# Moving the fourth attention element, the turned attention and two groups of transfers earlier or later in a hand-ordered graph network kernel

## The chip, the core and the metric

The kernel runs on one core of a Trainium2 chip. The core has a matrix engine (TensorE; PE in the profile, with its weight loads as PEld), three engines for elementwise work (VectorE or DVE, ScalarE or ACT, GpSimd or POOL) and SyncE (SP), whose queue issues every transfer of this kernel to 16 DMA engines. The engines run side by side and wait for one another through semaphores. Each queue takes its instructions strictly in program order, so an instruction that waits holds up everything behind it on that queue.

The metric is the device time of one execution in microseconds. The kernel before took 2347.32 us (median of 3 runs, 2341.13 to 2347.89).

## The reference: what is computed

The input x is 128 elements of 128 nodes with 512 features, and adj is one 128x128 matrix for all of them. Two layers are applied, both float32:

```python
# layer 0: normalise, graph convolution, residual
h = max(layernorm(x), 0)
x = x + norm_adj @ (h @ W0) + b0          # norm_adj: adj scaled by rsqrt of its row sums, both sides
# layer 1: normalise, attention with 8 heads of 64, residual
h = max(layernorm(x), 0)
q, k, v = h @ Wq + bq, h @ Wk + bk, h @ Wv + bv
scores = q @ k.T / 8 + (1 - adj) * -1e9
x = x + softmax(scores) @ v @ Wo + bo
```

## The kernel before, in words

**Groups and stages.** The 128 elements are cut into 32 groups of four (`GB`, `NG`). The kernel is a software pipeline over stages t. A stage has five blocks of TensorE work in this order: W (layer 0's weight product of group t+1), Q, K and V (the three projections of group t), and Y (the output projection of group t-1). Each block is a 512x512x512 product made by Strassen's scheme as seven smaller products, some of them split by a second Strassen level (`Projection.step`, L553). The seven give the places of a block their names: `Q0` to `Q6`. Between the seventh product of K and the first of V, at place `V0`, stand the attention products of group t-1 (`attend`, L929, elements in the order 2, 3, 0, 1) and the scores of group t (`scores`, L855, order 0, 1, 3, 2).

**The plan.** `at(stage, place, f, ...)` puts a step on a list, and `block` (L1146) runs the lists: steps of place `Q0` come ahead of that product, `Q0b` after the product and the reads that belong to its `step`, `Q0c` after the rest of its reads. The program order so made is the order on every queue. A place says nothing of time by itself: a step that is issued by SP or ACT runs when its queue reaches it and its semaphores are there.

**Operands of a product.** Strassen needs sums of blocks. `output_operands` (of the attention's output, tile `op_o`), `attention_operands` (of the second layer's h, `op_h`) and `gcn_operands` (of layer 0's, `op_a`) make them on POOL: four operations of 128x512 (L411 to L414) and nine of 128x256 (L94), some 11.7 us together. TensorE cannot go on to the second product of a block before the first of the small ones are done.

**Attention.** Element b of a group goes through these steps: scores with the mask added by DVE (element 3 instead is copied by ACT, L869, and masked by POOL, `add_mask`, L880); `row_max` (DVE, L884, 1.2 us); `exponentials` (ACT, L896, eight heads in two halves); `softmax_end` (a reciprocal on DVE, L901, and a multiplication on POOL, L907, 1.9 us). The weights are then transposed in two steps. `flip_att` (L909) transposes 32x32 squares on DVE (1.25 us) and writes 512 KB to DRAM in one transfer (`turned<-att`, L915). `turn_att` (L917) reads them back in four transfers of 128 KB in rows of 128 bytes (`att<-turned`, L786), which puts the squares in their places. SP may not issue these four before the write has landed. Five buffers hold all this: element b's weights go to the buffer of scores b-1, and its turned form to that of b-2, so element 0's turned form takes the buffer of element 3's scores and its flip waits for element 3's exponentials.

**The second layer's h** goes the same way: `flip_h` (L767) for elements 0 and 1 and for 2 and 3, one write each (`turned_h<-att`, `turned_h<-op_o`), and `turn_h` (L777). The second write leaves from slots 28 to 35 of tile `op_o`, which `output_operands` overwrites with its small operations.

**Weights** do not all fit: the four prepared weights (q, k, v, o) lie in DRAM and are loaded again in each stage into two buffers, five transfers of 512 KB each (`reload_w`, L1115, with places from `reloads_of`, L1128). In the block named by the key, the weights for the block after the next one are loaded.

**The last and first stages** have columns of their own in the list of steps (L975): `first` for t = 1, `final` for t = 31, `place` for t = 2 to 30. In stage 31 there is no W block on TensorE, so its places all come directly after Y.

Of the kernel before, what the change touches and what calls it, by code (L numbers as in the profile page):

```python
# [97 lines left out]
def kernel(  # L98
# [19 lines left out]
    H = 8  # L118
# [47 lines left out]
    def source(g, half):  # L166
        return staged.get((g, half)) if (g, half) in staged else xts[g, half]
# [507 lines left out]
    def ln1(g, half, js=(0, 1), ready=None):  # L675

        if (g, half) not in scale1:
            scale1[g, half] = Norm(source(g, half), f"1_{g}_{half}", g > 2)
        for j in js:
            scale1[g, half].statistics(j)  # L680
        if ready is None or ready:
            scale1[g, half].scale(ready or js)
# [282 lines left out]
    def at(slot, place, f, *args):  # L965
        plan.setdefault((slot, place), []).append((f, *args))

    for t in range(-1, NG + 1):
# [3 lines left out]
        if 0 <= t - 1 < NG - 1:  # L972
            g = t - 1

            for first, final, place, f, *args in (  # L975
                ("W4", "Q0b", "Q0b", flip_att, 0),
                ("W6", "Q2b", "Q3", turn_att, 0),
                ("Q3", "Q2", "Q2c", flip_att, 1),
                ("Q5", "Q4", "Q5", turn_att, 1),
                ("W6", "-Y3", "W2", exponentials, 2, 0, H // 2),  # L980
                ("Q1c", "-Y4", "W3", exponentials, 2, H // 2, H),
                ("Q4c", "-Y5b", "W4b", softmax_end, 2),
                ("Q6c", "-Y5", "W5", exponentials, 3, 0, H // 2),
                ("K0c", "-Y6", "W6", exponentials, 3, H // 2, H),
                ("K2c", "Q0b", "Q1c" if t == 2 else "Q0b", softmax_end, 3),
                ("K1", "Q3", "Q4b", flip_att, 2),
                ("K3", "Q4b", "Q5", flip_att, 3),
                ("K3", "Q5", "K0", turn_att, 2),
                ("K5", "Q6", "K1", turn_att, 3),
            ):  # L990
                place = first if t == 1 else final if last else place
                if f in (flip_att, turn_att) and turned_in_place(g, args[0]):
                    continue
                at(t - place.startswith("-"), place.strip("-"), f, g, *args)
            if t == 1:
                at(1, "K4", transpose_att, g, 2)
                at(1, "K5", transpose_att, g, 3)
            for b in (2, 3, 0, 1):
                at(t, "V0", attend, g, b)
        if t == 0:  # L1000

            at(0, "Q0b", ln2, 1, 0)
            at(0, "Q1b", ln2, 1, 1)
            at(0, "K6", norm_h, 1, 0)
            at(0, "K6", norm_h, 1, 1)
            at(0, "V4", transpose_h, 1, 0)
            at(0, "V4", norm_h, 1, 2)
            at(0, "V5", transpose_h, 1, 1)
            at(0, "V5", norm_h, 1, 3)
            at(1, "W0", transpose_h, 1, 2)  # L1010
            at(1, "W1", transpose_h, 1, 3)
            at(1, "W1b", attention_operands, 1)
            at(2, "Q5", attention_residual, 1, 0)
            at(2, "K1", attention_residual, 1, 1)
        elif 1 <= t + 1 < NG and t >= 0:
            g = t + 1
            at(t, "Q3b" if g < NG - 1 else "Q0b", ln2, g, 0)
            at(t, "K0b" if g < NG - 1 else "Q3b", ln2, g, 1)
            if g == NG - 1:

                places = ("Q3", "Q4", "Q5", "Q5", "Q6", "Q6", "K1", "K2", "K2")
                steps = ((norm_h, 0), (norm_h, 1), (transpose_h, 0), (norm_h, 2), (transpose_h, 1), (norm_h, 3))
                steps += ((transpose_h, 2), (transpose_h, 3))
            else:
                places = ("K1c", "K2c", "K4c", "K5b", "K3", "K4b", "K6b", "V0b", "Y5")
                if t == 1:
                    places = ("K2c", "K3c", "K6", "K6b", "K4b", "K5b", "V0b", "V0b", "Y5")
                steps = ((norm_h, 0), (norm_h, 1), (norm_h, 2), (norm_h, 3))
                steps += tuple((flip_h, b) for b in range(GB))
                for half in range(2):  # L1030
                    at(t, ("V3", "Y0")[half], turn_h, g, half)
            for place, (f, b) in zip(places, steps):
                at(t, place, f, g, b)
            at(t, places[8], attention_operands, g)
            at(t + 1, "Q3", attention_residual, g, 0)
            at(t + 1, "Q4", attention_residual, g, 1)
# [2 lines left out]
            at(t, "Y3" if t == NG else "Q3" if last else "W3", store_half, t - 2, 1)  # L1039
        if 3 <= t + 2 < NG:  # L1040
            at(t, "W0b" if t > 1 else "W0", load_x, t + 2, (0,), t > 1)
            at(t, "W1" if t > 1 else "W0", load_x, t + 2, (1,), t > 1)
        if 2 <= t + 2 < NG:
            g = t + 2
            if t > 0:
                at(t, "Q0b", ln1, g, 0, (0,), ())
                at(t, "Q1c", ln1, g, 0, (1,), (0, 1))
                at(t, "Q3b", ln1, g, 1)
            places = (("Q3", "Q5"), ("Q3", "Q6"), ("Q5b", "K1"), ("Q6", "K2"))
            if t == 1:  # L1050
                places = (("Q4", "K0"), ("Q4", "K1"), ("K0b", "K2"), ("K1b", "K3"))
            for b, (norm, mix) in enumerate(places):
                at(t, norm, gcn_norm, g, b)
                at(t, mix, gcn_mix, g, b)
            at(t, "K2" if t > 1 else "K4" if t > 0 else "V1b", gcn_operands, g)
            at(t, "Q6" if t > 1 else "Y1" if t > 0 else "K3", gcn_residual, g, 0)
            at(t, "K1" if t > 1 else "Y2" if t > 0 else "K3", gcn_residual, g, 1)
        if 0 <= t < NG:
            g = t
            for b in (0, 1, 3, 2):  # L1060
                at(t, "V0", scores, g, b)
            if t > 0:
                at(t, "V0c", output_operands, t - 1)
            at(t, "V1b", row_max, g, 0)
            at(t, "V3b", exponentials, g, 0, 0, H // 2)
            at(t, "V4b", exponentials, g, 0, H // 2, H)
            at(t, "V6", softmax_end, g, 0)
            if last:
                at(t, "V5b", row_max, g, 1)
                at(t, "V5b", exponentials, g, 1, 0, H // 2)  # L1070
                at(t, "V6", exponentials, g, 1, H // 2, H)
                at(t, "Y1b", softmax_end, g, 1)
                at(t, "Y2", transpose_att, g, 0)
                at(t, "Y4", transpose_att, g, 1)
            else:
                if t > 0:
                    at(t, "V3b", row_max, g, 1)
                    at(t, "Y1", exponentials, g, 1, 0, H // 2)
                    at(t, "Y2", exponentials, g, 1, H // 2, H)
                    at(t, "Y4", softmax_end, g, 1)  # L1080
                else:
                    at(t, "V4b", row_max, g, 1)
                    at(t + 1, "W2", exponentials, g, 1, 0, H // 2)
                    at(t + 1, "W3", exponentials, g, 1, H // 2, H)
                    at(t + 1, "Q1c", softmax_end, g, 1)
                at(t, "V6b", row_max, g, 2)
                at(*((t, "Y1") if t > 0 else (1, "Q3")), add_mask, g, 3)
                at(*((t, "Y3b" if g == NG - 2 else "Y6b") if t > 0 else (1, "Q5b")), row_max, g, 3)
        if last:
            g = t  # L1090
            at(t, "Y0", row_max, g, 2)
# [36 lines left out]
    def reloads_of(t):  # L1128

        when = {  # L1130
            "Q": ((t, "K2"), (t, "K2"), (t, "K2"), (t, "K2"), (t, "K3")),
            "K": ((t, "K5"), (t, "V0"), (t, "V0"), (t, "V0"), (t, "V0")),
            "V": ((t, "V3"), (t, "Y0"), (t, "Y0"), (t, "Y0"), (t, "Y3")),
            "Y": ((t, "Y4"), (t + 1, "W2"), (t + 1, "W2"), (t + 1, "W2"), (t + 1, "W3" if t + 1 < NG - 1 else "Q2c")),
        }
        if t == 1:

            when["K"] = ((1, "V0"),) * len(PARTS)
        for kind in "QKVY":
            if kind in "QKV" and t == NG:  # L1140
                continue
            reading[0] += 1
            for part, place in enumerate(when[kind]):
                at(*place, reload_w, reading[0] + 2, part)
# [10 lines left out]
    def prologue():  # L1155
# [71 lines left out]
        at(1, "Q3c", combine_w, "o", nc.gpsimd)  # L1227
        at(1, "Q5", combine_inner, "o", nc.gpsimd)
        at(1, "K3", keep_w, "o", (slice(0, 16), slice(16, SLOTS)))
        at(1, "K3", keep_w, "k")  # L1230
        at(1, "W0c", output_bias)
        at(1, "K1c", attention_residual, 0, 0)
        at(1, "K2c", attention_residual, 0, 1)

    with tc.manual_schedule(
        engines={
# [64 lines left out]
```

## Time and profile before

| quantity | value |
|---|---|
| median of 3 runs | 2347.32 us |
| the profiled execution, its own time | 2345.87 us |
| span of its profile | 2344.1 us |
| granted TensorE clock, mean | 0.993 |
| TensorE busy | 2232.0 us, 95% |
| VectorE, GpSimd, ScalarE busy | 80%, 80%, 55% |
| DMA: moved, rate | 599.23 MB, 256 GB/s |
| DMA: share of 16 engines, the kernel's own queue | 86.8% |
| median time from issue to landing: turned<-att, att<-turned, turned_h<-op_o, w<-wd_o | 4.1, 4.1, 8.9, 11.4 us |

How to read it: the span is from the first to the last instruction of the program, and the run's own time lies 1.8 us above it. A busy engine is one that executes, and an idle one is only of interest if the end waits for it. TensorE's 112 us without work are spread over 32 stages of about 71.5 us. The list of waits says who waited for whom. The timeline of SP says when transfers are issued: its rows show descriptors being made, not the data moving, and the landing comes some microseconds later. A table of stretches of the span (windows) gives the busy time of every engine and the share of the 16 DMA engines in each stretch.

### The profile page before, as it was taken

Reading aid. Unit: us, or ns where it says so; the run is one execution under the profiler, and the core shown is the slowest. Engines: PE = TensorE matmul, PEld = TensorE weight load, DVE = VectorE, ACT = ScalarE, POOL = GpSimd, SP = SyncE. Lnnn points to the kernel's source line nnn. Section 1 sums busy time; section 2 is a strip of 40 time slices with the busy share of each in tenths; the row PEclk is TensorE's granted clock in tenths of the full one; section 3 lists DMA queues with packets and bytes.
Section 4 is the critical chain, followed back from the end, with each engine's and each line's share of the span. In section 5 each row is a group of like instructions: output and inputs, shape, how many; then the busy total and the mean of one; then the engine's idle time right before and its main releaser. Section 6 shows DMA issues by size and latency. Waiting matters only on the chain.

```text
span 2344.1 us, 78627 instructions
## 1 busy us (share of the span) xinstructions
PE 2232.0 (95%) x31597; PEld 1885.5 (80%) x31597; DVE 1886.2 (80%) x4248; ACT 1290.9 (55%) x3821; POOL 1864.7 (80%) x1993
## 2 busy tenths in 40 slices
PE   9989999999999999999999999999999999999988
PEld 7778888888878888888888888888788888888777
DVE  7778887888888788888788887888788888878775
ACT  4556654665645655546656456565466564565434
POOL 7887978779878788788787787887887977877844
PEclk9999999999999999999999999999999999999999
DMA  5488899899899998899898898899999998998884
GB/s 155 142 276 257 240 284 290 249 259 263 259 284 286 241 281 239 273 289 265 251 264 252 282 286 241 276 240 275 291 255 263 261 256 280 289 251 270 225 240 146
DMA packets 908109, 599.23 MB, mean 256 GB/s; under 512 B 765665, under 2 KB 772961, under 8 KB 907105
## 3 DMA queue, kind: packets, MB, share of 16 engines
q1 hardware_dynamic: 907744, 594.20, 86.8%
q8 instruction: 250, 4.10, 0.7%
q14 instruction: 115, 0.93, 0.1%
HBM read 455.68 MB, written 138.41 MB: 253 GB/s over the span
## 4 chain that ended last, share of the span: by engine, by line
PE 53%; DMA 10%; POOL 9%; SPq 8%; DVE 8%; ACT 7%; issue 4%; POOLq 0%; DVEq 0%
PE bank_a L142 20%; PE bank_d L142 11%; SPq L786 8%; PE bank_c L142 6%; DMA turned_h<-op_o 6%; PE bank_b L142 6%; POOL op_o L94 4%; DMA att<-turned 4%; ACT q L808 3%; PE bank_d L865 3%; DVE v L478 3%; PE pa L142 2%; ACT unused L339 2%; PE po L940 2%; ACT unused L340 1%
## 5 line engine op out<-in xcount | busy, mean ns | idle before, releaser
L896 ACT ACTIVATE att<-att,nmx 128x128 f32<-128x128 f32 x1024 | 406.9, 504 | 230.5 <-DVE nmx L884 228.3
L94 POOL TENSOR_TENSOR op_o<-op_o 128x256 f32<-128x256 f32 x297 | 212.3, 739 | 211.4 <-DMA turned_h<-op_o 115.8
L142 PE MATMUL bank_a<-op_h,w 128*64 128x256 f32 x2976 | 355.1, 381 | 11.6 <-ACT q L808 11.6
L142 PEld LDWEIGHTS bank_a<-op_h,w 128*64 128x64 f32 x2976 | 206.1, 137 | 100.3 <-ACT q L808 18.6
L478 DVE TENSOR_TENSOR xt<-xt,bank_d 128x512 f32<-128x512 f32 x610 | 269.7, 467 | 11.8 <-PE bank_d L142 0.8
L907 POOL TENSOR_TENSOR att<-att,rsm 128x1024 f32<-128x1024 f32 x121 | 228.5, 1898 | 17.6 <-DVE rsm L901 14.7
L142 PE MATMUL bank_d<-op_h,w 128*64 128x128 f32 (+1 forms) x3424 | 221.7, 275 | 0.0
L94 POOL TENSOR_TENSOR op_a<-op_a 128x256 f32<-128x256 f32 x279 | 197.4, 731 | 15.1 <-ACT v L822 5.4
L808 ACT ACTIVATE q<-bank_a,bqk 128x256 f32<-128x256 f32 x192 | 79.7, 466 | 235.2 <-PE bank_a L142 235.1
L896 ACT ACTIVATION_READ_ACCUMULATOR att<-att,nmx 128x1 f32 x1024 | 208.2, 203 | 0.0
L142 PEld LDWEIGHTS bank_d<-op_h,w 128*64 128x64 f32 x3424 | 195.1, 137 | 6.7 <-issue 0.2
L94 POOL TENSOR_TENSOR op_h<-op_h 128x256 f32<-128x256 f32 x270 | 191.0, 731 | 9.4
L872 DVE SCALAR_TENSOR_TENSOR att<-bank_d,msk 128x512 f32<-128x512 f32 x128 | 82.4, 686 | 127.0 <-PE bank_d L865 127.0
L142 PE MATMUL bank_a<-w,op_o 128*64 128x256 f32 x1536 | 182.6, 380 | 0.0
L371 ACT ACTIVATE h<-xt,nb,rs 128x512 f32<-128x512 f32 x142 | 173.4, 1226 | 16.4 <-POOL nb L356 14.7
L142 PE MATMUL bank_a<-w,op_h 128*64 128x256 f32 x1488 | 178.0, 381 | 0.0
L142 PE MATMUL bank_a<-w,op_a 128*64 128x256 f32 x1488 | 176.5, 379 | 0.0
L493 DVE TENSOR_TENSOR xt<-bank_a,xt 128x512 f32<-128x512 f32 x252 | 166.5, 681 | 3.0 <-PE bank_a L142 3.0
L142 PE MATMUL bank_d<-w,op_o 128*64 128x128 f32 (+1 forms) x1768 | 127.9, 279 | 36.9 <-POOL op_o L94 36.8
L822 ACT COPY v<-bank_a 128x512 f32<-128x512 f32 x96 | 56.2, 585 | 180.0 <-PE bank_a L142 143.7
L884 DVE TENSOR_REDUCE nmx<-att 128x8 f32<-128x1024 f32 x128 | 153.9, 1203 | 0.0
L914 DVE STREAM_TRANSPOSE att<-att 128x1024 f32<-128x1024 f32 x122 | 152.5, 1250 | 1.5 <-ACT att L896 1.2
(198 smaller groups left out, 5916.5 us busy)
## 6 DMA issues: line engine op xcount, KB each, us to landing
w<-wd_v SPq DMA_DIRECT2D x155, 512.0 KB, 6.0
w<-wd_o SPq DMA_DIRECT2D x155, 512.0 KB, 11.4
w<-wd_q SPq DMA_DIRECT2D x150, 512.0 KB, 5.3
w<-wd_k SPq DMA_DIRECT2D x150, 512.0 KB, 8.6
turned<-att SPq DMA_DIRECT2D x122, 512.0 KB, 4.1
att<-turned SPq DMA_DIRECT2D x488, 128.0 KB, 4.1
out_dram<-xt SPq DMA_DIRECT2D x62, 512.0 KB, 6.0
op_h<-turned_h SPq DMA_DIRECT2D x232, 128.0 KB, 5.2
```

Of the source, the lines that this page charges most:

```text
L94: engine.tensor_tensor(twice(out), twice(x), twice(y), ALU.subtract if minus else ALU.add)
L142: nc.tensor.matmul(out[y : y + P // 2], lhsT[:, y : y + P // 2], rhs, **flags)
L371: nc.scalar.activation(dst, src, AF.Relu, bias=nb[:, j : j + 1], scale=rs[:, j : j + 1])
L478: nc.vector.tensor_tensor(dst, dst, src, f)
L493: nc.vector.tensor_tensor(t, src.rearrange("p (r f) -> p r f", r=2), t, ALU.add)
L786: nc.sync.dma_start(dst[:, :, y * 32 : (y + 1) * 32], rows[y])
L808: nc.scalar.activation(dst[:, r], src[:, r], AF.Identity, bias=bqk[:, i, oc : oc + 1], scale=1.0)
L872: nc.vector.scalar_tensor_tensor(dst, pss[p], SCALE, mask, ALU.mult, ALU.add)
L884: nc.vector.tensor_reduce(nmx, att_of(g, b), AX.X, ALU.max, negate=True)
L896: nc.scalar.activation(dst, src, AF.Exp, bias=nmx[:, h : h + 1], scale=1.0, accum_out=sm[:, h : h + 1])
L907: engine.tensor_tensor(att, att, rsm.unsqueeze(2).to_broadcast([P, H, P]), ALU.mult)
L914: nc.vector.transpose(dst, weights_of(g, b).rearrange(order, i=4))
```

## The change

For t = 2 to 30 (the column `place`) the change moves these steps; for t = 31 (the column `final`) most of them go earlier still.

- Element 3 of a group: its mask on POOL from Y1 to V4, its row maxima on DVE from Y6b (Y3b in stage 30) to Y2b, its exponentials from W5 and W6 to Y5 and Y6 of the stage before, its softmax end from Q0b to W2. Element 2's exponentials and softmax end also move from W places to Y places.
- The turned attention: flips from Q0b, Q2c, Q4b, Q5 to W0c, Q0b, Q2c, Q4b, and turns from Q3, Q5, K0, K1 to W2, Q2, Q4, Q6. On SP the order of writes (w) and turns (T) was w0 w1 T0 w2 T1 w3 T2 T3, and is now w0 T0 w1 T1 w2 T2 w3 T3, where w0 and T0 come ahead of the k weights.
- The second write of h (`flip_h` of element 3) from V0b to K6b, ahead of the scores on DVE, and on SP ahead of four of the five transfers of o's weights, which go from V0 to V0c.
- The k weights from W2 and W3 to W3 and W6, both loads of x to W0b, and `attention_operands` from Y5 to Y6b.
- In Q, one normalisation goes from Q3 to Q3b, one mix from Q5 to Q5b and one group's statistics from Q3b to Q3c.
- At the start: half 1 of group 3 takes its statistics on DVE rather than ACT, the prepared k weights are saved at Q6 rather than K3, and group 0's second residual bias is added (on DVE) at V4b and V5b rather than K1c and K2c.

```diff
-            scale1[g, half] = Norm(source(g, half), f"1_{g}_{half}", g > 2)
+            scale1[g, half] = Norm(source(g, half), f"1_{g}_{half}", g > 3 or g == 3 and half == 0)
...
             for first, final, place, f, *args in (
-                ("W4", "Q0b", "Q0b", flip_att, 0),
-                ("W6", "Q2b", "Q3", turn_att, 0),
-                ("Q3", "Q2", "Q2c", flip_att, 1),
-                ("Q5", "Q4", "Q5", turn_att, 1),
-                ("W6", "-Y3", "W2", exponentials, 2, 0, H // 2),
-                ("Q1c", "-Y4", "W3", exponentials, 2, H // 2, H),
-                ("Q4c", "-Y5b", "W4b", softmax_end, 2),
-                ("Q6c", "-Y5", "W5", exponentials, 3, 0, H // 2),
-                ("K0c", "-Y6", "W6", exponentials, 3, H // 2, H),
-                ("K2c", "Q0b", "Q1c" if t == 2 else "Q0b", softmax_end, 3),
-                ("K1", "Q3", "Q4b", flip_att, 2),
-                ("K3", "Q4b", "Q5", flip_att, 3),
-                ("K3", "Q5", "K0", turn_att, 2),
-                ("K5", "Q6", "K1", turn_att, 3),
+                ("W4", "-Y6b", "W0c", flip_att, 0),
+                ("W6", "W0", "W2", turn_att, 0),
+                ("Q3", "W0b", "Q0b", flip_att, 1),
+                ("Q5", "W4", "Q2", turn_att, 1),
+                ("W6", "-Y3", "-Y3", exponentials, 2, 0, H // 2),
+                ("Q1c", "-Y4", "-Y4", exponentials, 2, H // 2, H),
+                ("Q4c", "-Y5b", "-Y5b", softmax_end, 2),
+                ("Q6c", "-Y5", "-Y5", exponentials, 3, 0, H // 2),
+                ("K0c", "-Y6", "-Y6", exponentials, 3, H // 2, H),
+                ("K2c", "W0", "W2", softmax_end, 3),
+                ("K1", "Q0b", "Q2c", flip_att, 2),
+                ("K3", "Q1", "Q4", turn_att, 2),
+                ("K3", "Q2", "Q4b", flip_att, 3),
+                ("K5", "Q3", "Q6", turn_att, 3),
             ):
...
-                places = ("K1c", "K2c", "K4c", "K5b", "K3", "K4b", "K6b", "V0b", "Y5")
+                places = ("K1c", "K2c", "K4c", "K5b", "K3", "K4b", "K6b", "K6b", "Y6b")
...
-            at(t, "W1" if t > 1 else "W0", load_x, t + 2, (1,), t > 1)
+            at(t, "W0b" if t > 1 else "W0", load_x, t + 2, (1,), t > 1)
...
-                at(t, "Q3b", ln1, g, 1)
-            places = (("Q3", "Q5"), ("Q3", "Q6"), ("Q5b", "K1"), ("Q6", "K2"))
+                at(t, "Q3c", ln1, g, 1)
+            places = (("Q3", "Q5b"), ("Q3b", "Q6"), ("Q5b", "K1"), ("Q6", "K2"))
...
-                at(*((t, "Y1") if t > 0 else (1, "Q3")), add_mask, g, 3)
-                at(*((t, "Y3b" if g == NG - 2 else "Y6b") if t > 0 else (1, "Q5b")), row_max, g, 3)
+                at(*((t, "V4") if t > 1 else (1, "Y1") if t > 0 else (1, "Q3")), add_mask, g, 3)
+                at(*((t, "Y2b") if t > 1 else (1, "Y3b") if t > 0 else (1, "Q5b")), row_max, g, 3)
...
-            "K": ((t, "K5"), (t, "V0"), (t, "V0"), (t, "V0"), (t, "V0")),
+            "K": ((t, "K5"), (t, "V0c"), (t, "V0c"), (t, "V0c"), (t, "V0c")),
...
-            "Y": ((t, "Y4"), (t + 1, "W2"), (t + 1, "W2"), (t + 1, "W2"), (t + 1, "W3" if t + 1 < NG - 1 else "Q2c")),
+            "Y": ((t, "Y4"), (t + 1, "W3"), (t + 1, "W3"), (t + 1, "W3"), (t + 1, "W6" if t + 1 < NG - 1 else "Q2c")),
...
-        at(1, "K3", keep_w, "k")
+        at(1, "Q6", keep_w, "k")
...
-        at(1, "K1c", attention_residual, 0, 0)
-        at(1, "K2c", attention_residual, 0, 1)
+        at(1, "V4b", attention_residual, 0, 0)
+        at(1, "V5b", attention_residual, 0, 1)
```

More of the change, by code (lines that the diff above doesn't have):

```diff
@@ L1024 @@
             else:
-                places = ("K1c", "K2c", "K4c", "K5b", "K3", "K4b", "K6b", "V0b", "Y5")
+                places = ("K1c", "K2c", "K4c", "K5b", "K3", "K4b", "K6b", "K6b", "Y6b")
                 if t == 1:
-                    places = ("K2c", "K3c", "K6", "K6b", "K4b", "K5b", "V0b", "V0b", "Y5")
+                    places = ("K2c", "K3c", "K6", "K6b", "K4b", "K5b", "V0b", "V0b", "Y6b")
                 steps = ((norm_h, 0), (norm_h, 1), (norm_h, 2), (norm_h, 3))
@@ L1131, in reloads_of @@
             "Q": ((t, "K2"), (t, "K2"), (t, "K2"), (t, "K2"), (t, "K3")),
-            "K": ((t, "K5"), (t, "V0"), (t, "V0"), (t, "V0"), (t, "V0")),
+            "K": ((t, "K5"), (t, "V0c"), (t, "V0c"), (t, "V0c"), (t, "V0c")),
             "V": ((t, "V3"), (t, "Y0"), (t, "Y0"), (t, "Y0"), (t, "Y3")),
-            "Y": ((t, "Y4"), (t + 1, "W2"), (t + 1, "W2"), (t + 1, "W2"), (t + 1, "W3" if t + 1 < NG - 1 else "Q2c")),
+            "Y": ((t, "Y4"), (t + 1, "W3"), (t + 1, "W3"), (t + 1, "W3"), (t + 1, "W6" if t + 1 < NG - 1 else "Q2c")),
         }
         if t == 1:
-            when["K"] = ((1, "V0"),) * len(PARTS)
+            when["K"] = ((1, "V0c"),) * len(PARTS)
         for kind in "QKVY":
```

## The prediction, as it stood before the result was known

> **What bounds the kernel now.** I read the list of waits first, restricted to TensorE (columns: engine and tile <- who ended the wait: us in total, times, longest).
>
> ```profile
> PE po L940 <- DMA att<-turned: 40.1, 25, 5.9
> PE bank_d L142 <- POOL op_o L94: 36.8, 53, 7.5
> PE bank_a L142 <- ACT q L808: 11.6, 29, 2.4
> PE po L940 <- POOL op_a L94: 8.9, 5, 2.2
> ```
>
> The reader is to see three stalls that recur in every stage: attention waits for its turned weights (rows 1 and 4 are the same stall under two names, 49.0 us), Y1 waits for op_o (36.8), Q5 for q's read (0.33 each). A stage takes 71.5 us (28 stages, t = 3 to 30, between the landings of the last turned transfer), so TensorE alone would need some 68.5.
>
> Then the chain of waits around one stage, for what ends the first stall:
>
> ```profile
> 1073.43 3.80 DMA att<-turned
> 1077.23 0.35 issue
> 1077.58 1.09 PE po L940 x16
> ...
> 1145.16 3.32 DMA att<-turned
> ```
>
> The turned transfer lands at 1077.23, the next stage's at 1148.48, and TensorE starts at once behind it. So I look at what holds the transfers: the busy times in three stretches of this stage (last two columns: share of 16 DMA engines, GB/s).
>
> ```profile
> 1077.00:1124.00 47.00, 45.81 (x660) 39.11 (x662) 37.98 (x83) 21.30 (x84) 38.30 (x40) 1.00 0.97 322
> 1124.00:1128.00 4.00, 3.98 (x64) 3.35 (x60) 3.93 (x10) 2.59 (x6) 2.88 (x4) 1.00 0.16 63
> 1128.00:1148.00 20.00, 18.73 (x276) 15.91 (x272) 17.03 (x45) 16.41 (x32) 17.59 (x21) 1.00 0.96 178
> ```
>
> This is the main reading: the DMA engines are full for 47 us (weights, h, x, stores) and for the last 20 us (turned attention). A stage has about 4 us in which they rest, because SP stands at flips that DVE has not made yet. SP's timeline of the stage before shows the order in the last stretch (start, length of issue; x2 in the first row is the writes at 1050.10 and 1055.97):
>
> ```profile
> 1050.10 6.19 SPq L915 DMA_DIRECT2D turned<-att  x2
> 1056.39 3.14 SPq L786 DMA_DIRECT2D att<-turned  x4
> 1059.63 2.17 SPq L915 DMA_DIRECT2D turned<-att  x1
> 1061.91 3.12 SPq L786 DMA_DIRECT2D att<-turned  x4
> 1065.13 0.77 SPq L915 DMA_DIRECT2D turned<-att  x1
> 1065.99 8.19 SPq L786 DMA_DIRECT2D att<-turned  x8
> ```
>
> From the second row on a turn never stands right behind its own write; another turn lies between and covers the write's landing. The changed order does put each turn directly behind its write. The trace has that order once, in stage 1, with the DMA share of the pause in it:
>
> ```profile
> 113.51 3.05 SPq L786 DMA_DIRECT2D att<-turned  x4
> 116.66 0.67 SPq L915 DMA_DIRECT2D turned<-att  x1
> 120.33 3.33 SPq L786 DMA_DIRECT2D att<-turned  x4
> ...
> 119.50:121.50 2.00, 2.00 (x28) 1.50 (x26) 2.00 (x3) 0.00 (x0) 1.81 (x4) 1.00 0.08 27
> ```
>
> One pair takes 120.33 - 113.51 = 6.82 us, of which the DMA engines rest some 1.9 (0.08 busy in 2.0): SP can't issue the turn before the write has landed, and nothing else is in the queue.
>
> **The change part by part.**
>
> *Turned attention, one place sooner.* SP's order w0 w1 T0 w2 T1 w3 T2 T3 becomes w0 T0 w1 T1 w2 T2 w3 T3; w0 and T0 also pass a store and four k transfers. Behind a waiting turn stand on SP: behind T0 that store and the k transfers, behind T1 and T2 the next write, behind T3 v's five transfers; these land 2 to 8 us after the last turn, as before, and V's first product, at +6.7, wants the first of them, so they keep their cover. I count from the landing of the last turned transfer. From there to the landing of the last k transfer DMA work is continuous: median 46.5 us over the 28 stages (44.6 to 48.0 but for stage 30, which has no x to load). Into it goes the first pair, behind x, so it shifts the k transfers by 6.82. w1 is in the queue behind them (its flip, at Q0b, is done at about +44, the queue gets to it at +53), and three more pairs follow. Sum: 46.5 + 4 x 6.82 = 73.8 us, +2.3 on 71.5. By bounds: a pair can't be shorter than a write into an empty queue (1050.10 to its landing, 3.1) plus the issue of its turn (3.15), 6.25, which gives 71.5; at the second pair of stage 1 the last part landed 6.05 after its issue began, with 1.15 for the write 7.2, which gives 75.3. I take 6.82, the only one measured whole. Times 28: +64, ends 0 and +106.
>
> TensorE meanwhile needs 71.5 less the attention stall (1.5 a stage) less most of the next item, 69.5. So the stall that the change attacks comes back at the same instruction: attention of element 3 waits for the last turn, now 4 us a stage instead of 1.5.
>
> *h's second write ahead of o's weights.* The flip (0.70) moves on DVE ahead of the scores, where DVE idles 3.98 us (1006.37 to 1010.34). The write enters the queue after one o transfer instead of five, and lands four times 1.28 = 5 us sooner, at about +12.5. POOL is through L414 at +10.1 and needs 3.5 more for the five operations that Y1 wants at +19. POOL's wait (7.8 us in this stage) falls to 2.4, Y1's stall of 1.05 a stage is gone. o's last four transfers land 1.3 later, at +17.6, ahead of Y1. Cover: worth 1.05 x 28 = 29 if TensorE were the bound; behind a DMA bound, nothing.
>
> *Element 3's mask, maxima, exponentials.* Nothing is added. The mask (POOL, 2.38) ends at 1025.2 in the shown stage, ahead of its reader; queued behind it is element 0's softmax end, which nothing wants before W0c. The maxima (DVE, 1.21) now stand at Y2b, directly ahead of the four reads of bank d that end at 1032.16; TensorE writes bank d again from 1032.12. Late next is therefore bank d at Y4, by some 0.7 us a stage (1.21 less 0.4 to 0.6 of slack): that gives back two thirds of the 1.05. The first flip at W0c takes the place that the maxima leave at Y6b (1.25 for 1.21). ACT has 7.73 idle ahead of element 3's exponentials, so they cost nothing sooner. `attention_operands` comes behind element 2's softmax end, from 1036.58 to about 1038.9; its first five small operations end at 1047.8, and Q1 wants them at 1049; cover 1.2 us, and what it slips beyond falls on TensorE.
>
> *k transfers at W3 and W6, x at W0b.* The x loads keep their order on SP. k's last transfer lands at about +53, K0 begins at +55 and wants only the first part, which did not move: cover 2 us for K0, 4 for K1.
>
> *Q3b, Q5b, Q3c.* Element 0's mix (16 matmuls, 0.87) leaves its place ahead of Q5's product. Before, TensorE did it and then waited 0.33; now q's read is 0.8 earlier but the product waits for it in the open: 0.1 slower to 0.3 faster a stage, taken as 0.
>
> *Start.* Saving k's weights (13.5 us in the queue) moves from 137.8 to about 124, into a time when SP idles (126.3 to 135.8), so h's second write in stage 1 lands before 163.4 and Y1's 7.46 us stall there goes, with up to 3 us of half clock behind it; between -11 and 0 (if POOL's save is what SP waits for), taken as -8. Two statistics go from ACT (0.63 + 0.72 each) to DVE (0.66 + 0.18 each), two residual biases move on DVE: between -2 and +2, taken as 0.
>
> *Stage 31.* Its W places come at once after Y, so the pairs start at about 2254 and run one behind the other: w0 lands 2257, T0, w1, three k transfers (to 2268), T1, w2 lands 2273.5, T2, w3 2280.5. The last k transfer stands at Q2c behind T2 and w3 and lands at about 2282, where before it landed at 2272.3 and cost TensorE 2.5 us. So K4 waits 12 us. T3 lands at 2286.4 and is then hidden, so the 5.87 and 1.61 of attention and their slow clock go. Net: +2, between -12 (k in time) and +6.
>
> *Sum* against the profiled execution: 2345.9 + 64 - 8 + 2 = 2404; the median of the runs is 1.4 higher: 2405.
>
> **A rule against the rows.** The Trainium skill, page "Perfetto Trace Analysis", section "Identifying the Most-Contended Engine", takes the engine with the highest occupancy and for DMA the utilization of HBM. Against the page's 358 GB/s the measured 256 are 72%, under the 80% of TensorE's weight loads, so by the rule TensorE is the bound, both stalls are gain, and the sum would be some 2284 (rival 1). I go by the rows: 0.97 in 47 us.
>
> The second is the page "TensorE: Matmul & The Clock Gate": a gap beyond about 3.4 us halves the clock. The rows have 10.24 us at half clock behind 5.87 and 7.46 us of stall and 1.00 behind 2.0. Stalls of 4 lie between. By the rule each would cost at least 1.7 us of TensorE, 48 in all, if nothing covered it.
>
> By rows alone: TensorE's slack of 4 us covers a short spell; SP's store after Y6 has some 3 us before the queue runs dry, so a longer spell adds 0 to 1 us a stage.
>
> **The rivals.**
> 1. *TensorE is the bound, the change does what it says.* For it: TensorE is 95% busy, and w1's flip is 6 us earlier than w1 was needed. Against: the 0.97. Stage 69.5: 2345.9 - 2.0 x 28 - 8 + 2 = 2284. It is one mechanism: the full stretch from V to W shrinks because transfers in it no longer wait for TensorE. It breaks even where the stretch comes to 44.2 (71.5 - 4 x 6.82) and pays in full at 42.2; the smallest with x loads is 44.6.
> 2. *The pairs cost less*, and the 4 us that were idle pay for them. Pair 6.25 to 6.5, stage 71.5 to 72.5: 2345.9 - 6 + 0 to 28, and 1.4 for the median, 2341 to 2369. For it: the busy shares (47 x 0.97 + 4 x 0.16 + 20 x 0.96 = 65.4 us) and four pauses of 1.9 make 73.0, a little under 73.8. Against: DMA engines that lag behind the others in a full queue must all be waited for at each pause.
> 3. *The clock gate or bank d come on top*: 75.5 to 77 a stage, 2455 to 2495.
>
> **How the numbers follow.** Forecast 0.62 (stage 73.0 to 75.4: 2383 to 2452), rival 1 0.17, rival 2 0.14, rival 3 0.07. 0.3% is 7 us, about what a measurement can tell from no change. Faster: rival 1 and a fifth of rival 2, 0.20; same: 0.05; slower: 0.75. Range: without rival 3 and most of rival 1, 2325 to 2452; the likeliest's own is 2383 to 2452.
>
> **What would show it.** SP's timeline: every `att<-turned` row starts 3 to 7 us after its write, rows of x4 only. DMA share near zero for 1.5 to 2 us ahead of each. Attention's wait for `att<-turned` over 100 us in sum, Y1's for op_o below 10, `turned_h<-op_o` landing sooner, a wait for bank d or a DVE read at Y4, k's wait at stage 31. Wrong if a stage's full stretch is much shorter than 46.5, or if w1 lands before +54.

## The result, and the profile after

The changed kernel takes 2543.17 us (median of 4 executions, 2541.18 to 2551.26) where the kernel before took 2346.06 beside it (median of 4, 2341.13 to 2347.89): a ratio of 1.085, 95% interval 1.082 to 1.088. It is slower, as predicted, but by 197 us instead of 59; the predicted range ended at 2452. The profiled execution took 2541.18 us with a span of 2539.4, and a stage now takes 78.6 us (before 71.4, predicted 73.8; medians between the landings of the last turned transfer).

The waits of TensorE in the changed kernel (engine, line and tile <- who ended the wait: us in total, times, longest):

```profile
PE po L940 <- DMA att<-turned: 188.8, 48, 6.3
PE bank_a L142 <- ACT q L808: 23.0, 29, 2.4
PE bank_d L142 <- DVE xt L478: 17.1, 29, 0.6
PE bank_c L142 <- DMA w<-wd_k: 10.7, 1, 10.7
```

The wait for op_o is gone. Attention's wait for its turned weights has grown from 49.0 to 188.8 us and is most of what is left. What is late can be read from the end of the chain of waits of one stage, and from SP's timeline of the same stage (start, length of issue):

```profile
1314.02 3.88 DMA turned<-att
1318.49 0.66 SPq L786
1319.20 0.73 SPq L786
1319.97 3.55 DMA att<-turned
1323.65 1.97 PE po L940 x16
```

```profile
1282.10 0.34 SPq L915 DMA_DIRECT2D turned<-att  x1
1288.35 2.67 SPq L786 DMA_DIRECT2D att<-turned  x4
1291.12 1.23 SPq L958 DMA_DIRECT2D out_dram<-xt  x1
1292.45 2.35 SPq L1126 DMA_DIRECT2D w<-wd_k  x4
1294.90 0.58 SPq L915 DMA_DIRECT2D turned<-att  x1
1304.38 2.89 SPq L786 DMA_DIRECT2D att<-turned  x4
1307.37 0.74 SPq L915 DMA_DIRECT2D turned<-att  x1
1311.13 2.79 SPq L786 DMA_DIRECT2D att<-turned  x4
1314.02 0.86 SPq L915 DMA_DIRECT2D turned<-att  x1
1317.92 3.34 SPq L786 DMA_DIRECT2D att<-turned  x4
```

Each turn stands directly behind its own write, alone in rows of x4, and begins 3.8 to 9.5 us after the write was issued: SP waits for the write to land. The list of SP's own waits has one row for this, here as it stands before and in the changed kernel:

```profile
SPq L786 <- DMA turned<-att: 16.8, 3, 7.3
SPq L786 <- DMA turned<-att: 620.9, 122, 9.4
```

What the DMA engines do meanwhile is in these stretches of the stage, one ahead of each turn (us; busy time of PE, PEld, DVE, ACT, POOL; granted clock, share of 16 DMA engines, GB/s):

```profile
1287.10:1289.60 2.50, 2.50 (x36) 2.00 (x34) 2.36 (x6) 0.00 (x0) 2.50 (x5) 1.00 0.05 21
1302.40:1305.70 3.30, 3.30 (x50) 2.72 (x46) 3.19 (x10) 3.13 (x8) 2.69 (x4) 1.00 0.11 39
1310.40:1312.50 2.10, 2.10 (x28) 1.58 (x26) 2.10 (x8) 1.09 (x2) 2.10 (x2) 1.00 0.08 20
1317.20:1319.20 2.00, 1.25 (x23) 1.01 (x20) 2.00 (x8) 0.58 (x1) 1.92 (x3) 1.00 0.04 16
```

Four pauses of 2.0 to 3.3 us, in which by these shares the DMA engines rest 9.2 us in sum; the prediction had four times 1.9, 7.6. And behind the stall TensorE is slow. These two stretches begin where the last turn of the stage before has landed (1246.0):

```profile
1245.60:1249.20 3.60, 3.05 (x29) 3.08 (x31) 0.00 (x0) 0.58 (x1) 1.54 (x3) 0.50 0.94 358
1249.20:1252.60 3.40, 3.40 (x36) 3.07 (x35) 0.00 (x0) 1.17 (x2) 0.36 (x1) 0.59 1.03 324
```

The granted clock is 0.50 and then 0.59 over these 7 us. Over the run its mean is 0.956 (0.993 before).

### The profile page after: what moved, and what is told of

Its sections match the earlier page's. It is cut to its first block, busy times and chain, and to the rows that moved or that the text cites. A ratio compares the mean times of both kernels' runs of the same rounds, so it can differ in the third digit from the quotient of the medians.

```text
span 2539.4 us, 78841 instructions
## 1 busy us (share of the span) xinstructions
PE 2281.9 (90%) x31597; PEld 1937.7 (76%) x31597; DVE 1885.3 (74%) x4252; ACT 1288.3 (51%) x3813; POOL 1867.4 (74%) x1994
## 3 DMA queue, kind: packets, MB, share of 16 engines
q1 hardware_dynamic: 907744, 594.20, 80.2%
## 4 chain that ended last, share of the span: by engine, by line
PE 68%; DMA 13%; DVE 7%; ACT 5%; SPq 3%; issue 3%; POOL 1%; DVEq 0%; POOLq 0%
PE bank_a L142 25%; PE bank_d L142 14%; PE bank_c L142 7%; PE bank_b L142 7%; DMA turned<-att 6%; DMA att<-turned 4%; PE pa L142 4%; SPq L786 3%; PE bank_d L865 3%; PE po L940 2%; DVE xt L478 2%; ACT q L808 2%; PE bank_b L940 2%; DMA w<-wd_k 2%; PE bank_a L940 1%
## 5 line engine op out<-in xcount | busy, mean ns | idle before, releaser
L940 PE MATMUL po<-att,v 128*64 128x128 f32 x1024 | 95.0, 345 | 188.8 <-DMA att<-turned 188.8
L940 PEld LDWEIGHTS po<-att,v 128*64 128x64 f32 x1024 | 77.6, 176 | 199.8 <-issue 196.3
L411 POOL TENSOR_TENSOR op_o<-op_o 128x512 f32<-128x512 f32 x31 | 39.4, 1271 | 204.2 <-ACT op_o L406 204.2
L406 ACT COPY op_o<-po 128x512 f32<-128x512 f32 x62 | 36.2, 585 | 282.1 <-PE po L940 281.8
```

The costliest lines, as they stand in the source:

```text
L940: nc.tensor.matmul(po[p * HD : (p + 1) * HD, c * P : (c + 1) * P], vs[g][:, b, h * HD : (h + 1) * HD], aT[:, p * NC + c, :], start=True, s ...
```

## The experiments

Stage times and landings named below are medians over the same 28 stages of each trace (a landing is the time at which a transfer's data has arrived). The kernel before was timed beside every group of runs: 2341.4 us (x1 to x4), 2339.6 (x5 to x8), 2342.9 (x9, x10) and 2339.4 (x11, x12).

**Is it the turned attention? One part undone (x1), one part alone (x2).** x1 is the changed kernel with the flips and turns at their places of before; x2 is the kernel before with the new flips and turns and the steps of elements 2 and 3 that go with them.

```diff
# x1, against the changed kernel
-                ("W4", "-Y6b", "W0c", flip_att, 0),
-                ("W6", "W0", "W2", turn_att, 0),
+                ("W4", "Q0b", "Q0b", flip_att, 0),
+                ("W6", "Q2b", "Q3", turn_att, 0),
...
```

> The changed kernel with the flips and turns alone put back to the places of before; every other step stays moved (element 3's mask, maxima and exponentials, h's second write, o's, k's and x's transfers, the steps in Q). Theory A (each turn stands on SP directly behind its own write, the DMA engines rest in between, and the stage becomes bound by transfers): the loss goes. 2346 less 29 (op_o's stall in Y1) plus 17 (0.59 a stage at Y4 behind the maxima) plus 11 (q's wait 0.74 instead of 0.33) is 2345; 2325 to 2360. Rival B (the other moved steps, on DVE, POOL, ACT or in the order of the weight transfers, cost the time): it stays above 2450.

Measured: 2306.5 us, ratio 0.985 (0.983 to 0.987): 1.5% faster than the kernel before, and 18.5 us below the lower end of theory A's range. The rest of the change is worth more than the expectation counted; x8 below shows which part.

> The kernel before with the attention part alone: flips and turns at the new places, and element 3's mask, maxima and exponentials early, which the first flip needs; h's writes, the weights, x and the steps in Q stay. Theory A: most of the 197 us are here, 2500 to 2560, with the stall of op_o in Y1 back but hidden. Rival B: under 2430.

Measured: 2566.3 us in one execution, 6 above theory A's range. So the places of the flips and turns make all of the loss, and more: what else is in the change is a gain of some 35 us. x2 is a little slower still: its row maxima of element 3 now wait on DVE for the mask (51.6 us in sum for POOL's result; POOL still stands at h's late write first), and bank d's reads stand behind them:

```profile
PE bank_d L142 <- DVE xt L478: 70.8, 29, 2.9
```

**Is it the order on SP, or that everything is earlier? (x3)** Flips as in the changed kernel, every turn one write later, so that SP's order is w0 w1 T0 w2 T1 w3 T2 T3:

```diff
-                ("W6", "W0", "W2", turn_att, 0),
-                ("Q5", "W4", "Q2", turn_att, 1),
-                ("K3", "Q1", "Q4", turn_att, 2),
+                ("W6", "W0c", "Q2", turn_att, 0),
+                ("Q5", "Q1", "Q4", turn_att, 1),
+                ("K3", "Q2b", "Q5", turn_att, 2),
```

> The changed kernel with its early flips, but each turn stands one write later on SP (w0 w1 T0 w2 T1 w3 T2 T3, turns at Q2, Q4, Q5, Q6), so that a write's landing is covered by other transfers. Theory A: the stage has no pauses, the attention is early, TensorE is the bound: about 69.5 us a stage, 2270 to 2310, faster than before. Rival B, and rival D (the DMA engines are full anyway, and any earlier attention transfer only delays k's): 2350 or more.

Measured: 2286.9 us, ratio 0.977 (0.975 to 0.979), a stage of 69.5. The waits of TensorE in x3 no longer hold attention at all:

```profile
PE bank_a L142 <- ACT q L808: 23.0, 29, 2.4
PE bank_d L142 <- DVE xt L478: 19.6, 29, 2.9
PE bank_c L142 <- DMA w<-wd_k: 9.7, 1, 9.7
```

It is the order: with the same early flips, a turn directly behind its own write costs 256 us against a turn one write later.

**Do the four pairs cost alike? (x4, x6)** x4 moves the first turn alone, from W2 to W6c, behind the store and the k transfers; x6 leaves the first and moves the other three as in x3.

```diff
# x4, against the changed kernel
-                ("W6", "W0", "W2", turn_att, 0),
+                ("W6", "W0", "W6c", turn_att, 0),
```

> The changed kernel with one turn moved: the first one from W2 to W6c, behind the store and k's four transfers, so that these run while its write lands. Theory A: one pause of 1.9 us of four is filled, 28 stages: 2470 to 2510, and the other three stay. Rival E (k's transfers, held up behind the first turn, are what costs): under 2430. Rival D (work is only reordered): 2530 to 2550.

> The changed kernel with the first turn left directly behind its write, ahead of the store and the k transfers, and the other three one write later (w0 T0, k, w1 w2 T1 w3 T2 T3). If the four pairs cost alike (the prediction's sum), three of four pauses go: some 2350 to 2380 us. If the first pair carries most of the loss, because the k transfers and the next writes stand behind it (moving it alone was worth 153 us of 256), most stays: 2420 to 2500 us, with attention's wait for att<-turned still over 80 us.

Measured, in one execution each: x4 2389.9 us (stage 72.4), x6 2372.2 us (stage 72.1). Neither theory holds: x4 fell where the first pair carries most of the loss, x6 where the pairs cost alike. The first pair, undone alone, gives 6.2 us a stage; the other three together 6.5. From the last k transfer to the last turn it is some 22 us in the changed kernel and 16 in x6, so a pause between pairs is worth some 2.0, nearly what was predicted (1.9). The first pair is worth about as much as the other three. (A part of either gain is TensorE's clock, of which more below: its mean rose to 0.986 in x4 and 0.987 in x6.) The two gains don't add up, since at 69.5 TensorE takes over (x3: none of its longest waits is for a turn). If they did, the transfers alone would need 78.6 - 6.2 - 6.5 = 65.9 us a stage; that is an estimate, and near to the work that the DMA engines do in any of these kernels (86.8% of 2344.1 us before, 80.2% of 2539.4 after, both some 2035 us, 64 in each of 32 stages).

**What was the bound before? (x8)** The kernel before, with h's second write and nothing else of the change (the last two lines are stage 1's part of it):

```diff
-                places = ("K1c", "K2c", "K4c", "K5b", "K3", "K4b", "K6b", "V0b", "Y5")
+                places = ("K1c", "K2c", "K4c", "K5b", "K3", "K4b", "K6b", "K6b", "Y5")
...
-            "K": ((t, "K5"), (t, "V0"), (t, "V0"), (t, "V0"), (t, "V0")),
+            "K": ((t, "K5"), (t, "V0c"), (t, "V0c"), (t, "V0c"), (t, "V0c")),
...
-            when["K"] = ((1, "V0"),) * len(PARTS)
+            when["K"] = ((1, "V0c"),) * len(PARTS)
```

> The kernel before, with h's second write ahead of four of o's five weight transfers and nothing else of the change. The stall of Y1 for op_o (1.05 us in 28 stages) should go. If TensorE bounds the stage, that is 29 us: 2310 to 2325. If the DMA engines bound it, as the prediction read it, the gain is nothing: 2337 to 2350.

Measured: 2282.3 us, ratio 0.975 (0.973 to 0.978): 57 us faster, twice the larger of the two expected gains. The waits of TensorE in x8:

```profile
PE po L940 <- DMA att<-turned: 28.5, 25, 6.6
PE bank_a L142 <- ACT q L808: 11.6, 29, 2.4
PE po L940 <- POOL op_a L94: 7.9, 5, 2.0
```

The 36.8 us for op_o are gone, and attention's wait fell from 49.0 to 36.4 with the same transfers in the same order of writes and turns. The store behind Y leaves 29.5 us after the last turn instead of 31.1. The last k transfer lands almost where it did (46.0, before 46.5), so the full stretch of the DMA engines got hardly shorter; what did is the time from there to the last turn, 23.4 instead of 25.3 (medians of each), the part in which SP stands at flips. The stall at Y1 was a link of a loop: last turn, attention, V, Y, flips, writes, turns. The DMA engines did not bound the kernel before. In the two profiles the 63 us of span are, near enough, the 36.8 of this wait (7.5 of them in stage 1), 12.6 of attention's, and 15.5 less busy time of TensorE (2232.0 to 2216.5); about half of the last is clock (mean 0.993 to 0.996), the other half is not explained.

**The slow clock (x5, x10, x11, x12).** x5 gives TensorE eight products more in the stall, whose result attention overwrites; x11 four. x10 and x12 are the same two with the maxima of element 3 behind the reads of bank d (Y2c) and the steps of Q at their old places.

```diff
# x11, against the changed kernel, in attend (x5: range(8))
+        if b == 3 and 1 < g < NG - 1:
+            for _ in range(4):
+                nc.tensor.matmul(po, ident, vs[g][:, 2, :], start=True, stop=True)
```

> The changed kernel with eight extra products, about 0.5 us each by the rows of this case's 128x128 products (0.06 us for 64x128 columns), written into attention's own bank ahead of element 3's attention and then overwritten: TensorE has some 4 us of work in the 5.7 us in which it waited there. Nothing else is moved. If the half clock behind the stall delays the Y block, its store and so the transfers of the next stage (TensorE's half-clock time is 224 us in the changed kernel, 33 in the one before), the time falls by 1.5 to 3 us a stage: 2458 to 2503 us, with half-clock time under 60 us. If TensorE's slack covers the half clock, as the prediction had it (0 to 1 us a stage), it stays within 2520 to 2551. If the extra work itself delays attention, it rises above 2551.

Measured: 2537.5 us in one execution, clock 0.994. That looks as if the slow clock cost nothing. But eight products were too many. In x10's timeline of TensorE, where one last turned transfer landed at 1147.94, attention begins 1.6 us later, behind them:

```profile
1144.76 4.88 PE L939 MATMUL po<-v,ident 128*128 128x512 f32 x11
1149.58 0.66 PE L943 MATMUL po<-att,v 128*64 128x128 f32 x8
```

So V began 8.1 us after the landing instead of 8.5 (6.7 before), and the stage was 0.5 shorter. The test had put one delay in the place of another, and x11 mends that.

> The changed kernel with the stall filled with products as before, and the maxima of element 3 behind the reads of bank d and the steps of Q at their old places: TensorE reaches the end of Y about 1.0 us sooner in each stage, and so does the store that heads the next transfers. If that lateness is a link of the chain that sets the stage (it was read as 1.4 us of the 4.6 by which the stage came out longer than predicted), the time falls by 28 us from the filled kernel's 2537: 2503 to 2518. If the transfers alone set the stage, it stays within 2528 to 2545.

Measured: 2527.2 us in one execution, 10 below x5 and just below the second expectation; with the surplus of products in it, it decides little.

> The changed kernel with four extra products in the stall instead of eight. With eight, TensorE was at full speed but the extra products ended 1.4 us behind the landing of the last turn in each stage, so that V began only 0.5 us sooner than in the changed kernel (8.1 instead of 8.5 us behind that landing; 6.7 in the kernel before), and the stage was 0.5 us shorter. Four end ahead of the landing. If the half clock behind the stall is a link of the chain, one for one, V begins at about +6.7 and the stage is 1.9 us shorter: 2482 to 2500 us. If the transfers alone set the stage, 2528 to 2545.

Measured: 2499.0 us, ratio 1.066 (1.060 to 1.071); V begins at +6.7 and the stage is 77.0. The stretch behind a landing (1222.9) in x11:

```profile
1222.50:1226.10 3.60, 3.05 (x52) 2.91 (x54) 0.00 (x0) 1.35 (x3) 0.72 (x1) 1.00 0.96 363
```

In the same 3.6 us the clock is 1.00 and 52 products were done instead of 29. Against the changed kernel V begins 1.8 us sooner behind the landing, the store behind Y leaves 1.8 sooner (30.7 instead of 32.5), and the stage is 1.5 shorter: what TensorE loses to the slow clock, the store and the transfers behind it lose too, nearly one for one. That is 44 us in sum, and no less than that, since x11 still has a slow spell in some stages (mean clock 0.986, x5 0.994).

> The same four extra products, and the maxima of element 3 behind the reads of bank d and the steps of Q at their old places (0.59 and 0.41 us a stage of TensorE). If what TensorE loses between the landing and the store is handed on one for one, the wait for bank d (0.59) comes off too: 12 to 20 us below the kernel with four products alone, 2465 to 2486. If only the clock matters, no more than 5 below it. If the transfers alone set the stage, both stay within 2528 to 2545.

Measured: 2499.6 us in one execution, the same as x11, and the store behind Y leaves at the same +30.7. So the 12 to 20 us do not come, and the waits for bank d and q are off the chain in the changed kernel, or nearly so: the stage is 76.8 instead of 77.0, and with x11's own four executions 11 us apart a gain of a few us can't be told from none.

**A better version (x7, x9).** x7 is x3 with small moves taken back. Its result is not the reference's, though the amount of work is the same; the likely reason, which is not shown, is the last k transfer of stage 31, which x9 leaves where x3 has it. So its time only points to x9.

> The kernel with early flips and turns one write behind (2286.9 us), with four of the change's small moves taken back or shifted: the statistics and the mix in Q at their old places (wait for q 0.74 to 0.33 a stage: -12 us), the row maxima of element 3 behind the reads of bank d instead of ahead of them (Y2c; 0.59 a stage to 0: -17), the last k transfer of stage 31 at W6 instead of Q2c (-5 to -10), group 0's second residual bias at its old places (4.41 us stall in stage 1: -4). If TensorE is the bound, all of it is gain: 2245 to 2260 us. If the transfers bound it at about 69 us a stage, the stage moves take nothing off and it stays within 2270 to 2285.

Measured: 2269.2 us, just below the second expectation. The waits that the stage moves were to remove are gone; the k transfer is no gain, as TensorE then waits for it 16.0 us instead of 9.7. x9 leaves that transfer where it was and puts two turns of stage 31 behind it:

```diff
# x9, against x3
-                at(t, "Q3c", ln1, g, 1)
-            places = (("Q3", "Q5b"), ("Q3b", "Q6"), ("Q5b", "K1"), ("Q6", "K2"))
+                at(t, "Q3b", ln1, g, 1)
+            places = (("Q3", "Q5"), ("Q3", "Q6"), ("Q5b", "K1"), ("Q6", "K2"))
...
-                at(*((t, "Y2b") if t > 1 else (1, "Y3b") if t > 0 else (1, "Q5b")), row_max, g, 3)
+                at(*((t, "Y2c") if t > 1 else (1, "Y3b") if t > 0 else (1, "Q5b")), row_max, g, 3)
...
-        at(1, "V4b", attention_residual, 0, 0)
-        at(1, "V5b", attention_residual, 0, 1)
+        at(1, "K1c", attention_residual, 0, 0)
+        at(1, "K2c", attention_residual, 0, 1)
...
-                ("K3", "Q2b", "Q5", turn_att, 2),
-                ("K5", "Q3", "Q6", turn_att, 3),
+                ("K3", "Q3", "Q5", turn_att, 2),
+                ("K5", "Q4", "Q6", turn_att, 3),
```

> The kernel with early flips and turns one write behind (2286.9 us), with the statistics and the mix in Q at their old places (12 us by the wait for q), the row maxima of element 3 behind the reads of bank d (17 us by the wait for bank d), group 0's second residual bias at its old places (0 to 4), and in stage 31 the turns of elements 2 and 3 behind the last k transfer instead of ahead of it (7 to 10 by the wait for w<-wd_k). If TensorE is the bound of a stage, the sum is 2244 to 2258 us. If the transfers take over as the bound once TensorE needs a microsecond less, the first two are not gained: 2270 to 2280.

Measured: 2262.7 us (5 executions), ratio 0.966 (0.964 to 0.967): 80 us faster than the kernel before and 280 faster than the changed one. It is between the two expectations, 5 us above the upper end of the first. Most of the 80 us is not the early transfers: h's write alone (x8) gives 57 of them. What is left of TensorE's waits:

```profile
PE bank_a L142 <- ACT q L808: 11.6, 29, 2.3
PE bank_c L142 <- DVE xt L478: 6.3, 2, 4.4
PE bank_c L142 <- DMA w<-wd_k: 5.3, 1, 5.3
```

The wait for bank d is gone as expected, q is back at 0.33 a stage, and stage 31's wait is nearly halved: 35 us of waits less than in x3, of which 24 show in the time. The 4.4 us stall for bank c in stage 1 stayed, so the two residual biases were not its cause.

## Why the prediction was right in direction and wrong in size

The landings of one stage, in us behind the last turned transfer, beside what the prediction's sum says:

| landing of | before | predicted | changed | x11 (slow clock mostly gone) |
|---|---|---|---|---|
| second x load | 39.3 | 39.3 | 40.5 | 40.0 |
| last k transfer | 46.5 | 53.3 | 56.4 | 55.8 |
| next last turn | 71.4 | 73.8 | 78.6 | 77.0 |

The stage came out 4.8 us above the sum, which is 134 of the 138 us by which the forecast was missed. By the table the 4.8 are: x later by 0.7, the first pair longer by 1.8, the last three by 0.7, and 1.6 by the slow clock. Items 2 and 3 are the steps that failed.

1. *SP's order makes each turn wait for its own write, and the DMA engines rest.* Right. It is in SP's rows and in the four pauses, and x3 took the order alone back.

2. *"46.5 + 4 x 6.82 = 73.8".* This step failed: it priced the four pairs alike, and put the first one "behind x, so it shifts the k transfers by 6.82". The last three take some 22 us (21.2 with the slow clock mostly gone) against 20.5, near enough. The first was taken as 6.82 and costs 1.8 more in x11, and nearly all of that is in what stands behind it. It is the only one of the four with other transfers behind it ahead of the last turn: one store and four k transfers, each of 512 KB. These five take 8.9 us from the first turn's landing to the last k's in the changed kernel and in x11, 8.7 in x6, but 7.0 in the kernel before (from the second x load's landing) and 6.6 in x4 (from w0's landing), where no turn stands ahead of them. The pause does not explain it. The five transfers of v behind the last turn (also 512 KB each) take 8.2 us from its landing in the kernel before and 8.3 in x6, where that turn does not stand directly behind its own write, and 8.3 in the changed kernel, where it does and the engines rest ahead of it. So five large transfers behind a turn take longer than five behind other large transfers, and the trace of before had that price. Why a turn does this stays open.

3. *"a longer spell adds 0 to 1 us a stage".* This step failed too, and the sum took the 0. The cover that I named (TensorE's slack, 3 us of queue ahead of the store) was not there: x11 shows 1.5 a stage, 44 us. The prediction had quoted a rule for this and set it aside. The Trainium skill, page "TensorE: Matmul & The Clock Gate", section "Part 1: The HAM clock gate", says that the clock falls to half after an idle window of about 3.4 us; the prediction's estimate from it was at least 1.7 us a stage, 48 in all. The trace agrees (a clock of 0.50 behind stalls of up to 6.3 us), and the measured 44 is near it.

4. *"the DMA engines are full for 47 us": the main reading.* Wrong as the bound of the kernel before. x8 has the same transfers and 69.4 us a stage. The evidence was in the rows I showed: the 4 us of rest in each stage, in which SP stood at flips, say that the transfers were waiting for TensorE and DVE, and so that every stall ahead of those flips counts. It was also in the page of before, in the part on the chain that ended last (shares of the span by engine, then by line), which I did not use:

```profile
PE 53%; DMA 10%; POOL 9%; SPq 8%; DVE 8%; ACT 7%; issue 4%; POOLq 0%; DVEq 0%
PE bank_a L142 20%; PE bank_d L142 11%; SPq L786 8%; PE bank_c L142 6%; DMA turned_h<-op_o 6%; PE bank_b L142 6%; POOL op_o L94 4%; DMA att<-turned 4%; ACT q L808 3%; PE bank_d L865 3%; DVE v L478 3%; PE pa L142 2%; ACT unused L339 2%; PE po L940 2%; ACT unused L340 1%
```

`DMA turned_h<-op_o` and `POOL op_o` make 10% of it: h's second write was on the path that set the end. "Behind a DMA bound, nothing" should have been 57 us (x8). In the changed kernel that gain is there (no wait for op_o) but buried under the turns.

5. *Rivals.* Rival 1 was right that TensorE's stalls were the gain to be had in the kernel before, and wrong on the change. That its 2284 us is what x8 (2282) and x3 (2287) take is in part chance: it took both recurring stalls off at their own length, and x8 takes off one and gains twice that one's length. Rival 3 (2455 to 2495) was the nearest, with the right mechanism in the clock; bank d, its other part, is off the chain or nearly so (x12).

6. *Smaller steps.* Right: the wait for bank d, 0.59 a stage for some 0.7; stage 31's wait for k, 10.7 us for 12; op_o's wait gone. Wrong: Q's moves, taken as 0, raised the wait for q from 0.33 to 0.74 a stage. The waits for bank d and q cost little or nothing in the changed kernel (x12); in x3, where TensorE is the bound, they are some 31 us of waiting that x9 no longer has.

## What to carry to other kernels

When a queue runs strictly in order, put something else between a write and the read-back that waits for it: with another write there the changed kernel takes 2287 us instead of 2543. The early transfers themselves are worth little: the kernel before with h's write alone takes 2282. Before a full queue is called the bound, look at where it runs dry and for whom it then waits: that engine's stalls are part of the loop, and may be worth more than their own length (here 1.05 us gave 2.0). And a filler put in to test the cost of a stall must be shorter than the stall, or it measures itself.

## What was not expected of the hardware

Beside the stall of 1.05 us that was worth 2.0: a stall of 5 to 6 us at one instruction cost 1.5 us more behind it through the half clock, in each of 28 stages, and the later waits of the same stage did not absorb it: those for q and bank d are 23.0 and 17.1 us in sum with the slow clock, and 23.3 and 17.1 in x11. And five transfers of 512 KB that take 6.6 to 7.0 us behind other large transfers took 8.2 to 8.9 behind a turn, which reads 128 KB a transfer in rows of 128 bytes, with a pause ahead of it or without.
